# Three row strips side by side, and x, gathers and sums of the first product moved forward

## The chip, the cores and the metric

The kernel runs on one core of a Trainium2 chip. The metric is the device time of an execution in microseconds. The kernel before took 468.69, 468.70 and 470.52 us in three runs, a median of 468.7. One more execution was recorded by the hardware profiler.

## The reference

x has 32 batches of 128 tokens with 512 features. A mask marks up to 32 tokens at the end of each batch. A first half (two small networks) changes only the masked tokens, and a second half, a feed-forward network, changes all of them:

```python
shift, scale, gate_msa = split(silu(t) @ ada_w + ada_b, 3)
norm = where(m, layernorm(x) * (1 + scale) + shift, 0)
fwd = gelu(norm @ ssm_w1 + ssm_b1) @ ssm_w2 + ssm_b2
bwd = gelu(norm @ bwd_w1 + bwd_b1) @ bwd_w2 + bwd_b2
x = x + gate_msa * where(m, fwd + bwd, 0)
shift_mlp, scale_mlp, gate_mlp = split(silu(t) @ ffada_w + ffada_b, 3)
h = gelu_tanh((layernorm(x) * (1 + scale_mlp) + shift_mlp) @ ff_w1 + ff_b1)
out = x + gate_mlp * (h @ ff_w2 + ff_b2)
```

ff_w1 is 512 x 1024 and ff_w2 is 1024 x 512; all is float32. The flips of the reference cancel, token by token.

## The kernel before, in words

*The first half* works on slots. The masked tokens of all batches are numbered, and the first 512 of them fill four tiles of 128 slots, s0 to s3. A matrix `pick` says which batch each slot belongs to, in three copies, each on 32 partitions of its own. The rows of x are gathered by indirect DMAs of GpSimd (`gather_slots`, L270), two tiles at a time. The modulation of all batches (`mod1`: shift in partitions 0 to 31, scale in 32 to 63, gate in 64 to 95) is made once, and `slot_part` (L304) multiplies one of the three strips with that strip of `pick`, so that each slot has its batch's row; each such product takes a PSUM bank of the pool `ps_o` (three banks, tag "o") or `ps_h` (three banks). `modulated` (L177) normalises a tile with two VectorE instructions, which read scale and shift from PSUM. `transposed_slots` (L186) turns it, `hidden` (L193) makes eight blocks of 128 hidden features for two tiles at once, and `project` (L209) multiplies them with w2. For s0 and s1 `finish_slots` (L317) adds gate, bias and x, and writes the rows to `x1_wide` (with mean and variance beside them) and `x1_rows` in DRAM. For s2 and s3 this is done by `with_bias`, `with_gate` and `with_x` (L1246 to L1255), and `with_x` issues the write to `x1_rows`.

*The second half* takes the batches in four pairs, p = 0 to 3, of two sides of four batches. The rows of x are loaded and the masked ones overwritten by gathers from `x1_wide` (pair 0) or `x1_rows` (the others): `take_first_half` (L729), eight indirect DMAs on GpSimd. A gather waits for the load of its tile and for the writes of the rows. `load_side` (L345) loads one side, two transfers of 512 KB on SP's queue.

Both matrix products of the network are made with seven multiplications in place of eight, and the first product twice, one level inside the other. *Outer sums* of the tokens' features are `TokenBlocks.one(j)` (L836; j = 1 to 4, VectorE, 128 x 1024 each), *inner sums* `token_sums(j, n)` (L893; j = 1 to 4, and n = 0 to 3 for the blocks). Sums of the weights (`weight_sums`, L621) are stored to `t_rows` in DRAM (`store_weight_sums`, L633), and `load_weights` (L915) brings them back as `tw`. Outer products run in the order 1, 2, 5, 6, 3, 7, 4, each with inner products P1 to P7. One inner product is a phase of four matmul records (`phase`, L965). `window` (L1063) interleaves phases of two outer products: P5 and P1 of the new one, P3 and P7 of the old one, P2 and P6 of the new one, P4 of the old one. After P5 ScalarE copies the result p5; `with_p5` (L1022) adds it to a kept result on GpSimd; after P6 VectorE adds that to the bank in which P3 goes on accumulating. `fw2_of.combine` makes the sums of ff_w2 that the second product needs.

*Order.* Instructions stand in each engine's queue in the order in which the code names them, and each engine takes its own strictly in that order; a wait holds all that is behind it. Between L1257 and L1301 the order of the first pair is written out by hand; from the loop on it is set by `put(window, phase, function)`, which hangs a function behind a phase. Tiles come from pools with a fixed number of buffers: the tile `spare` (L607) holds sums of weights until they are stored, and the second pair's x goes into it; the other two tiles of that x take the buffers of the gathered slot rows `xc`. PSUM banks turn in the same way, and an allocation waits until the bank's last reader is done. SP issues nearly all direct DMAs, in order.

Of the kernel before, what the change touches and what calls it, by code (L numbers as in the profile page):

```python
# [22 lines left out]
def kernel(  # L23
# [153 lines left out]
    def modulated(src, scale, shift, name, t, stats=None):  # L177

        if stats is None:
            mv, rstd = statistics([src], name)  # L180
            stats = mv[:, 0, 0:1], rstd
        nc.vector.scalar_tensor_tensor(t, src, stats[0], scale, ALU.subtract, ALU.mult)
        nc.vector.scalar_tensor_tensor(t, t, stats[1], shift, ALU.mult, ALU.add)
        return t
# [119 lines left out]
    def slot_part(at, j, pool, tag):  # L304
        return of_slots(pick, at, mod1, j, pool, tag, f"part{j}_s{at}")
# [227 lines left out]
    modulation_matmuls(pm, ada_a, 0, 2, range(KC - 1))  # L533
    gather_slots(find_slots(1, (ps_h, "h")))
    modulation_matmuls(pm, ada_a, 0, 2, range(KC - 1, KC))
    modulation_rows(pm, mod1, modb_a, 0, 2)
    rows = [(slot_part(c, 1, ps_o, "o"), slot_part(c, 0, *((ps_o, "o"), (ps_h, "h"))[c])) for c in range(2)]
    xT_s = ssm.tile([P, KC, NH], F32, tag="xT", name="xT_s0", bufs=2)
    xT_t = ssm.tile([P, KC, NH], F32, tag="xT", name="xT_s1", bufs=2)
    xn = group_of_tiles("s")  # L540
    xn_s = [modulated(xc[c], *rows[c], f"s{c}", xn[:, c]) for c in range(2)]
    fw1 = fwp.tile([P, KC, FF], F32, name="fw1")
# [10 lines left out]
    ada_f = load_ada(ffada_w, "f", 3 * D)  # L553
    for t, vec in ((modb_f, ffada_b), (fb2, ff_b2)):
        broadcast_rows(t, vec, nc.sync)
    nc.sync.dma_start(fw2, ff_w2.rearrange("(k p) f -> p k f", p=P))
    ph_s = {}
# [15 lines left out]
    transposed_slots(xn_s[0], xT_s[:, :, ts(0, P)], "s0")  # L573
    gate_parts = tp.tile([P, D], F32, tag="t", name="gate_parts")
    pm = ps_o.tile([P, 512], F32, tag="o", name="pm_g")
    for k in range(KC):
        nc.tensor.matmul(
            pm[ts(k, B), :], sT[:, k, :], ada_a[:, k, ts(2, D)], start=True, stop=True
        )
    nc.scalar.copy(gate_parts, pm)  # L580
    ptr = ps_t.tile([P, 512], F32, tag="tr", name="ptr_b")
# [4 lines left out]
    nc.vector.tensor_copy(slot_i, ptr[:, n_bias : n_bias + B])  # L586
    hidden_of_tile(0, 0)
    pm = ps_o.tile([P, 512], F32, tag="o", name="pm_gate")
    nc.tensor.matmul(pm[ts(2, B), :], strips, gate_parts, start=True, stop=True)
    modulation_rows(pm, mod1, modb_a, 2, 3)  # L590
    hidden_of_tile(1, 0)
    transposed_slots(xn_s[1], xT_s[:, :, ts(1, P)], "s1")
    hidden_of_tile(2, 0)
# [72 lines left out]
    for f in range(3):  # L666
# [3 lines left out]
        h1.append(t)  # L670
    gs = [keep_gate(c, slot_part(c, 2, ps_o, "o")) for c in range(2)]
    mv_t, rstd_t = statistics(xc[2:], "s23")
    nc.vector.tensor_tensor(b2, b2, b2b, ALU.add)
    b2_row = dram.tile([1, D], F32, name="b2_row")
    for c in range(2):
        with_gated_bias(c, gs[c])
    Weights(fw1, KC // 2, FF // 2, t_1).combine(0, 1, 2, 3)
    h1 += hidden(xT_s, NH, w1, 0, AF.Gelu, "s0", ssm, range(3, HC))
    finish_slots(0, h1, gs[0])
# [5 lines left out]
    finish_slots(1, h1, gs[1])  # L685
    nc.sync.dma_start(b2_row, b2[0:1, :])

    rows = [(slot_part(2 + c, 1, ps_o, "o"), slot_part(2 + c, 0, ps_h, "h")) for c in range(2)]
    mod2 = const.tile([3 * B, D], F32, name="mod2")
    pm = ps_o.tile([P, 512], F32, tag="o", name="pm_f")  # L690
    modulation_matmuls(pm, ada_f, 0, 3, range(KC))
    xn_late = ssm.tile([P, 2, D], F32, tag="xT", name="xn_s_late", bufs=2)
    for c in range(2):
        t = modulated(
            xc[2 + c], *rows[c], f"s{2 + c}", xn_late[:, c], (mv_t[:, c, 0:1], rstd_t[:, c : c + 1])
        )
        transposed_slots(t, xT_t[:, :, ts(c, P)], f"s{2 + c}")
    modulation_rows(pm, mod2, modb_f, 0, 3)
# [506 lines left out]
    take_first_half(0, x_of[0], range(2 * G))  # L1205
    store_weight_sums(1)
    xT = [new_xT(0, side) for side in range(2)]
# [20 lines left out]
    def turn(k):  # L1228
        return lambda: transposed(1, xn_b, xT[1], k)
# [7 lines left out]
    after[4].insert(0, normalised_of_side_0)  # L1237
    after[7] += [lambda: weight_sums(4), normalised_of_side_1]
    h1 = hidden(xT_t, NH, w1, 0, AF.Gelu, "s1", ssm, after=after)
# [16 lines left out]

    po_s2 = project(0, h1, w2, "s2", {2: turn(0), 4: turn(1), 6: turn(2), 7: turn(3)})  # L1257
    of_x[0] = TokenBlocks(0, xT)
    of_x[0].one(1)
    fw2_of.combine(0, 1)  # L1260
    nc.vector.tensor_tensor(fb2_step, fb2[:, D // 2 :], fb2[:, : D // 2], ALU.subtract)
    with_bias(2, po_s2)
    with_gate(2, gs[0])
    with_x(2)
    po = project(1, h1, w2, "s3", bank=(ps_h, "h"))

    store_weight_sums(4, 2)
    with_bias(3, po)
    with_gate(3, gs[1])
    first_half.close()  # L1270
    hp = straight.enter_context(tc.tile_pool(name="hp", bufs=1))
    gp = straight.enter_context(tc.tile_pool(name="gp", bufs=1))
    now = FirstProduct(0, of_x[0].cut(), of_w)
    for j in (1, 2):
        now.load_weights(j)
    now.apart(1)
    for j in (2, 3):
        of_x[0].one(j)
    now.do(1, "P1")
    now.seed(1)  # L1280
    now.do(2, "P1")
    now.do(1, "P5", "P2", "P6")
    of_x[0].one(4)
    now.do(2, "P5")
    now.seed(2)
    now.do(1, "P7")
    now.with_p5(2, "22")
    now.token_sums(1, 0)
    with_x(3)
    x_of[1] = load_x(1, spare)  # L1290
    now.token_sums(1, 1)
    now.do(1, "P3")
    now.with_p5(2, "12")
    now.do(2, "P2", "P6")
    for n in range(2, 4):
        now.token_sums(1, n)
    for n in range(2):
        now.token_sums(2, n)
    now.do(1, "P4")
    for n in range(2, 4):  # L1300
        now.token_sums(2, n)  # L1301
    for p in range(NP):
# [25 lines left out]
        if more_pairs:  # L1328
# [18 lines left out]

            put(*((1, 6) if p else (2, 3)), take_first_half, p + 1, x_next, range(G))
            put(2, 6, take_first_half, p + 1, x_next, range(G, G + 2))
            put(3, 4, take_first_half, p + 1, x_next, range(G + 2, G + 3))  # L1350
            put(5, 4, take_first_half, p + 1, x_next, range(G + 3, 2 * G))
            for i, at in enumerate(((3, 1), (3, 3), (3, 4), (3, 6))):
# [196 lines left out]
```

## Time and profile before

| | |
|---|---|
| median of three runs | 468.7 us |
| profiled execution: time / span | 469.94 / 468.2 us |
| TensorE busy | 452.0 us, 97% |
| VectorE busy | 335.4 us, 72% |
| ScalarE busy | 176.4 us, 38% |
| GpSimd busy | 157.9 us, 34% |
| DMA | 70.95 MB, 152 GB/s on the mean |

The busy time of TensorE takes in half-filled stretches and a slower clock, so a busy engine is not one at its peak. The slots' last projection ends, and the first product begins, at 91.68 us of the span; the second product of pair 0 begins at 138.63 us. In a row of the order of time stand the start, the length, the engine, the line, the operation with the tile written and the tiles read, and in brackets the idle time ahead of it and what ended it.

### The profile page before, as it was taken

What the parts mean: (1) busy time and instruction counts of PE and PEld (TensorE: products, weight loads), DVE (VectorE), ACT (ScalarE), POOL (GpSimd) and SP (SyncE); (2) the same over time, 40 slices, a digit from 0 to 9 for tenths busy, and PEclk for the clock granted to TensorE, in tenths of its full rate; (3) what the DMA queues carried; (4) which work ended last, traced back from release to release, by engine and by line L of the source; (5) the groups of instructions that cost most, each with busy time, mean ns of one, the idle gap of its engine ahead of it and who ended that gap; (6) DMA issues with size and microseconds to landing.
All of it is one profiled execution on the core that took longest, in us unless ns stands there. A gap on an engine that the chain in (4) does not pass through costs nothing.

```text
span 468.2 us, 5888 instructions
## 1 busy us (share of the span) xinstructions
PE 452.0 (97%) x2026; PEld 368.4 (79%) x2026; DVE 335.4 (72%) x549; ACT 176.4 (38%) x381; POOL 157.9 (34%) x147
## 2 busy tenths in 40 slices
PE   6899999999799999999999999999999999999995
PEld 2385377577688888888888888888888887888884
DVE  4678876899469956997687499967873996433645
ACT  3131033544265074254543723544536144562000
POOL 4220171026985000289730004897000025660000
PEclk9899999999899999999999999999999999999999
DMA  8999926194314670944066529230863342212022
GB/s 285 392 392 390 340 96 99 39 357 157 105 66 160 112 114 33 332 149 162 3 202 100 104 88 335 86 142 2 225 96 85 125 168 74 84 77 104 0 81 103
DMA packets 82755, 70.95 MB, mean 152 GB/s; under 512 B 63136, under 2 KB 63664, under 8 KB 81698
## 3 DMA queue, kind: packets, MB, share of 16 engines
q1 hardware_dynamic: 67874, 58.47, 39.7%
q0 software_dynamic: 4064, 10.54, 6.5%
q10 hardware_dynamic: 10784, 1.52, 2.2%
q8 instruction: 17, 0.28, 0.3%
q14 instruction: 16, 0.13, 0.1%
HBM read 56.84 MB, written 13.70 MB: 151 GB/s over the span
## 4 chain that ended last, share of the span: by engine, by line
PE 90%; DVE 3%; DMA 2%; POOL 2%; issue 1%; SPq 0%; ACT 0%; POOLq 0%; DVEq 0%; ACTq 0%
PE a_o L1161 23%; PE e_o L1161 18%; PE a_m L974 17%; PE e_m L974 13%; PE po_s L216 6%; PE ph_s L199 5%; DMA x<-in_x_dram 2%; PE ph_s L564 1%; PE part_s L299 1%; PE pm_ss L279 1%; POOL x L733 1%; PE pm_f L279 1%; PE last L1161 1%; DMA mask_u<-in_mask_BxS_bk_dram 0%; POOL xc L254 0%
## 5 line engine op out<-in xcount | busy, mean ns | idle before, releaser
L1025 POOL TENSOR_TENSOR ha<-p_m,ha 128x512 f32<-128x512 f32 x20 | 26.2, 1310 | 151.4 <-ACT ha L1032 142.0
L1161 PE MATMUL e_o<-fw,ha 128*128 128x256 f32 x256 | 57.9, 379 | 0.0
L796 ACT ACTIVATE xT<-xT,modT 128x128 f32<-128x128 f32 x112 | 44.2, 480 | 31.7 <-DMA xT<-xn 31.6
L1161 PE MATMUL a_o<-t,hb 128*128 128x256 f32 x240 | 54.1, 379 | 0.0
L1161 PEld LDWEIGHTS e_o<-fw,ha 128*128 128x128 f32 x256 | 48.6, 190 | 6.6
L1161 PEld LDWEIGHTS a_o<-t,hb 128*128 128x128 f32 x240 | 45.6, 190 | 6.2
L936 ACT ACTIVATE hb<-hb,biasT 128x256 f32<-128x256 f32 x64 | 29.0, 501 | 28.8 <-POOL hb L1058 19.3
L1025 POOL TENSOR_TENSOR hb<-p_m,hb 128x512 f32<-128x512 f32 x20 | 29.1, 1453 | 27.2 <-DVE hb L1004 26.9
L988 ACT COPY p_m<-e_m 128x512 f32<-128x512 f32 x27 | 15.8, 585 | 47.9 <-PE e_m L974 46.4
L733 POOL DMA_INDIRECT x<-x_rows,slot_i x24 | 28.7, 1194 | 11.9 <-issue 10.6
L1032 ACT COPY ha<-e_m 128x512 f32<-128x512 f32 x32 | 18.5, 578 | 30.9 <-PE e_m L974 27.7
L1161 PE MATMUL a_o<-t,s 128*128 128x256 f32 x128 | 28.9, 379 | 0.0
L1161 PE MATMUL a_o<-fw,ha 128*128 128x256 f32 x128 | 28.9, 379 | 0.0
L1161 PE MATMUL e_o<-fw,s 128*128 128x256 f32 x128 | 28.9, 379 | 0.0
L999 DVE TENSOR_TENSOR e_m<-a_m,ha 128x512 f32<-128x512 f32 x20 | 13.9, 697 | 20.4 <-POOL ha L1025 9.5
L216 PE MATMUL po_s<-w,h_s 128*128 128x512 f32 x64 | 28.5, 592 | 0.0
L1161 PEld LDWEIGHTS a_o<-t,s 128*128 128x128 f32 x128 | 24.3, 190 | 3.3
L1161 PEld LDWEIGHTS a_o<-fw,ha 128*128 128x128 f32 x128 | 24.3, 190 | 3.3
L1161 PEld LDWEIGHTS e_o<-fw,s 128*128 128x128 f32 x128 | 24.3, 190 | 3.3
L936 ACT ACTIVATE ha<-e_m,biasT 128x256 f32<-128x256 f32 x48 | 20.0, 468 | 14.5 <-PE e_m L974 12.0
L974 PE MATMUL a_m<-xT,tw 128*128 128x256 f32 x96 | 24.6, 379 | 0.0
L1004 DVE TENSOR_TENSOR hb<-a_m,hb 128x512 f32<-128x512 f32 x20 | 13.7, 685 | 14.3 <-PE a_m L974 14.3
(226 smaller groups left out, 904.6 us busy)
## 6 DMA issues: line engine op xcount, KB each, us to landing
tw<-t_rows SPq DMA_DIRECT2D x16, 896.0 KB, 5.3
x<-in_x_dram SPq DMA_DIRECT2D x16, 512.0 KB, 7.5
gate<-gate_rows POOLq DMA_DIRECT2D x8, 1024.0 KB
out_dram<-x SPq DMA_DIRECT2D x15, 512.0 KB, 3.9
xT<-xn SPq DMA_DIRECT2D x92, 64.0 KB, 2.4
fw<-in_L_cond_ff_w_dram SPq DMA_DIRECT2D x2, 2048.0 KB
ada_f<-in_L_cond_ffada_w_dram SPq DMA_DIRECT2D x4, 768.0 KB, 16.2
ada_a<-in_L_cond_ada_w_dram SPq DMA_DIRECT2D x4, 512.0 KB, 3.7
```

The costliest lines, as they stand in the source:

```text
L199: nc.tensor.matmul(ph[:, :n], w[:, k, ts(f, P)], xT[:, k, :], start=(k == 0), stop=(k == KC - 1))
L216: nc.tensor.matmul(po, h[f][:, ts(i, P)], w[:, f, :], start=(f == 0), stop=(f == HC - 1))
L733: nc.gpsimd.indirect_dma_start(out=raw[i // 2][:, i % 2] if p == 0 else xs[i // G][i % G // 2][:, i % 2], out_offset=None, in_=x1_rows if ...
L796: nc.scalar.activation(out, src, AF.Identity, bias=shift, scale=scale)
L936: nc.scalar.activation(dst[:, n], src[:, n], AF.Gelu_apprx_tanh, bias=biasT[:, f : f + 1])
L974: nc.tensor.matmul(bank[:, ts(n, QT)], self.w_block(j, product)[:, ts(n, P)], self.x_block(j, product), start=(product in ("P1", "P5") and ...
L988: nc.scalar.copy(p5, e)
L999: nc.vector.tensor_tensor(e, a, p5, add)
L1004: nc.vector.tensor_tensor(dst, a, dst if prior else self.p5[j], add)
L1025: nc.gpsimd.tensor_tensor(self.place(RESULT[j], c), self.p5[j], other, ALU.add)
L1032: nc.scalar.copy(self.place(RESULT[j], c), src)
L1161: nc.tensor.matmul(part, src[:, k, ts(i, P)], w[product][:, k, :], start=(last and k == 0), stop=True, skip_group_check=True,)
```

## The change

Names are as above.

- The gates' matmuls `pm_g` stand in front of the first tile's transposes, in a bank of `ps_t`. The statistics of s0 are issued ahead of the second pair of `gather_slots`.
- `fb2` and `fw2` are loaded behind the writes of the first slot rows instead of with the other weights.
- `gate_and_next_tile(c)` makes the gate of tile c and scale and shift of tile 2 + c together, in three banks of `ps_o`, and normalises tile 2 + c at once, into `spare[1]`. It is called before hidden block 3 and behind block 6. The transposes of s2 and s3 then stand ahead of `pm_f`.
- Of the weight sums, `normalised_of_side_1` goes ahead of the fourth, all three stores stand together behind it, and behind these the loads of the second pair's first side. The first `turn` stands ahead of the projection of s2.
- The outer sums `one(2)` to `one(4)` are made before `with_bias(3)`, `with_x(3)` directly behind `with_gate(3)`, then the loads of the second side, and only then those of `tw`. The inner sums (1, n) come ahead of the first phase, (2, n) together behind `with_p5(2, "22")`. The combination of ff_w2 moves behind the phases written out by hand.
- All eight `take_first_half` of the second pair stand behind `with_p5(2, "12")` instead of in windows 2, 3 and 5.

```diff
-    gather_slots(find_slots(1, (ps_h, "h")))
+    token_i = find_slots(1, (ps_h, "h"))
     modulation_matmuls(pm, ada_a, 0, 2, range(KC - 1, KC))
     modulation_rows(pm, mod1, modb_a, 0, 2)
     rows = [(slot_part(c, 1, ps_o, "o"), slot_part(c, 0, *((ps_o, "o"), (ps_h, "h"))[c])) for c in range(2)]
+    gate_parts = tp.tile([P, D], F32, tag="t", name="gate_parts")
+    pm = ps_t.tile([P, 512], F32, tag="tr", name="pm_g")
+    for k in range(KC):
+        nc.tensor.matmul(
+            pm[ts(k, B), :], sT[:, k, :], ada_a[:, k, ts(2, D)], start=True, stop=True
+        )
+    nc.scalar.copy(gate_parts, pm)
...
-    xn_s = [modulated(xc[c], *rows[c], f"s{c}", xn[:, c]) for c in range(2)]
+    mv, rstd = statistics(xc[:1], "s0")
+    gather_slots(token_i)
+    xn_s = [
+        modulated(xc[0], *rows[0], "s0", xn[:, 0], (mv[:, 0, 0:1], rstd)),
+        modulated(xc[1], *rows[1], "s1", xn[:, 1]),
+    ]
...
-    for t, vec in ((modb_f, ffada_b), (fb2, ff_b2)):
-        broadcast_rows(t, vec, nc.sync)
-    nc.sync.dma_start(fw2, ff_w2.rearrange("(k p) f -> p k f", p=P))
+    broadcast_rows(modb_f, ffada_b, nc.sync)
...
     transposed_slots(xn_s[0], xT_s[:, :, ts(0, P)], "s0")
-    gate_parts = tp.tile([P, D], F32, tag="t", name="gate_parts")
-    pm = ps_o.tile([P, 512], F32, tag="o", name="pm_g")
...
-    nc.scalar.copy(gate_parts, pm)
...
     hidden_of_tile(0, 0)
+    hidden_of_tile(1, 0)
+    transposed_slots(xn_s[1], xT_s[:, :, ts(1, P)], "s1")
     pm = ps_o.tile([P, 512], F32, tag="o", name="pm_gate")
     nc.tensor.matmul(pm[ts(2, B), :], strips, gate_parts, start=True, stop=True)
     modulation_rows(pm, mod1, modb_a, 2, 3)
-    hidden_of_tile(1, 0)
-    transposed_slots(xn_s[1], xT_s[:, :, ts(1, P)], "s1")
     hidden_of_tile(2, 0)
...
-    gs = [keep_gate(c, slot_part(c, 2, ps_o, "o")) for c in range(2)]
     mv_t, rstd_t = statistics(xc[2:], "s23")
+    xn_late = []
+
+    def gate_and_next_tile(c):
+        gs.append(keep_gate(c, slot_part(c, 2, ps_o, "o")))
+        rows = slot_part(2 + c, 1, ps_o, "o"), slot_part(2 + c, 0, ps_o, "o")
+        xn_late.append(
+            modulated(
+                xc[2 + c], *rows, f"s{2 + c}", spare[1][:, c], (mv_t[:, c, 0:1], rstd_t[:, c : c + 1])
+            )
+        )
+
+    gs = []
+    gate_and_next_tile(0)
     nc.vector.tensor_tensor(b2, b2, b2b, ALU.add)
     b2_row = dram.tile([1, D], F32, name="b2_row")
-    for c in range(2):
-        with_gated_bias(c, gs[c])
+    with_gated_bias(0, gs[0])
+    h1 += hidden(xT_s, NH, w1, 0, AF.Gelu, "s0", ssm, range(3, HC - 1))
+    gate_and_next_tile(1)
     Weights(fw1, KC // 2, FF // 2, t_1).combine(0, 1, 2, 3)
-    h1 += hidden(xT_s, NH, w1, 0, AF.Gelu, "s0", ssm, range(3, HC))
+    with_gated_bias(1, gs[1])
+    h1 += hidden(xT_s, NH, w1, 0, AF.Gelu, "s0", ssm, range(HC - 1, HC))
     finish_slots(0, h1, gs[0])
...
     nc.sync.dma_start(b2_row, b2[0:1, :])
-
-    rows = [(slot_part(2 + c, 1, ps_o, "o"), slot_part(2 + c, 0, ps_h, "h")) for c in range(2)]
+    broadcast_rows(fb2, ff_b2, nc.sync)
+    nc.sync.dma_start(fw2, ff_w2.rearrange("(k p) f -> p k f", p=P))
+
+    for c in range(2):
+        transposed_slots(xn_late[c], xT_t[:, :, ts(c, P)], f"s{2 + c}")
     mod2 = const.tile([3 * B, D], F32, name="mod2")
     pm = ps_o.tile([P, 512], F32, tag="o", name="pm_f")
     modulation_matmuls(pm, ada_f, 0, 3, range(KC))
-    xn_late = ssm.tile([P, 2, D], F32, tag="xT", name="xn_s_late", bufs=2)
-    for c in range(2):
-        t = modulated(
-            xc[2 + c], *rows[c], f"s{2 + c}", xn_late[:, c], (mv_t[:, c, 0:1], rstd_t[:, c : c + 1])
-        )
-        transposed_slots(t, xT_t[:, :, ts(c, P)], f"s{2 + c}")
     modulation_rows(pm, mod2, modb_f, 0, 3)
...
     take_first_half(0, x_of[0], range(2 * G))
-    store_weight_sums(1)
...
-    after[7] += [lambda: weight_sums(4), normalised_of_side_1]
+    after[7] += [
+        normalised_of_side_1,
+        lambda: weight_sums(4),
+        lambda: store_weight_sums(1, 2, 4),
+        lambda: x_of.update({1: [load_side(1, 0, spare), None]}),
+        turn(0),
+    ]
...
-    po_s2 = project(0, h1, w2, "s2", {2: turn(0), 4: turn(1), 6: turn(2), 7: turn(3)})
+    po_s2 = project(0, h1, w2, "s2", {2: turn(1), 4: turn(2), 6: turn(3)})
     of_x[0] = TokenBlocks(0, xT)
     of_x[0].one(1)
-    fw2_of.combine(0, 1)
-    nc.vector.tensor_tensor(fb2_step, fb2[:, D // 2 :], fb2[:, : D // 2], ALU.subtract)
     with_bias(2, po_s2)
     with_gate(2, gs[0])
     with_x(2)
     po = project(1, h1, w2, "s3", bank=(ps_h, "h"))
-
-    store_weight_sums(4, 2)
+    for j in (2, 3, 4):
+        of_x[0].one(j)
     with_bias(3, po)
     with_gate(3, gs[1])
+    with_x(3)
     first_half.close()
...
+    x_of[1][1] = load_side(1, 1)
     now = FirstProduct(0, of_x[0].cut(), of_w)
     for j in (1, 2):
         now.load_weights(j)
+    for n in range(4):
+        now.token_sums(1, n)
     now.apart(1)
-    for j in (2, 3):
-        of_x[0].one(j)
     now.do(1, "P1")
     now.seed(1)
     now.do(2, "P1")
     now.do(1, "P5", "P2", "P6")
-    of_x[0].one(4)
     now.do(2, "P5")
     now.seed(2)
     now.do(1, "P7")
     now.with_p5(2, "22")
-    now.token_sums(1, 0)
-    with_x(3)
-    x_of[1] = load_x(1, spare)
-    now.token_sums(1, 1)
+    for n in range(4):
+        now.token_sums(2, n)
     now.do(1, "P3")
     now.with_p5(2, "12")
+    take_first_half(1, x_of[1])
     now.do(2, "P2", "P6")
-    for n in range(2, 4):
-        now.token_sums(1, n)
-    for n in range(2):
-        now.token_sums(2, n)
     now.do(1, "P4")
-    for n in range(2, 4):
-        now.token_sums(2, n)
+    fw2_of.combine(0, 1)
+    nc.vector.tensor_tensor(fb2_step, fb2[:, D // 2 :], fb2[:, : D // 2], ALU.subtract)
...
-            put(*((1, 6) if p else (2, 3)), take_first_half, p + 1, x_next, range(G))
-            put(2, 6, take_first_half, p + 1, x_next, range(G, G + 2))
-            put(3, 4, take_first_half, p + 1, x_next, range(G + 2, G + 3))
-            put(5, 4, take_first_half, p + 1, x_next, range(G + 3, 2 * G))
+            if p:
+                put(1, 6, take_first_half, p + 1, x_next, range(G))
+                put(2, 6, take_first_half, p + 1, x_next, range(G, G + 2))
+                put(3, 4, take_first_half, p + 1, x_next, range(G + 2, G + 3))
+                put(5, 4, take_first_half, p + 1, x_next, range(G + 3, 2 * G))
```

More of the change, by code (lines that the diff above doesn't have):

```diff
@@ L573 @@
     transposed_slots(xn_s[0], xT_s[:, :, ts(0, P)], "s0")
-    gate_parts = tp.tile([P, D], F32, tag="t", name="gate_parts")
-    pm = ps_o.tile([P, 512], F32, tag="o", name="pm_g")
-    for k in range(KC):
-        nc.tensor.matmul(
-            pm[ts(k, B), :], sT[:, k, :], ada_a[:, k, ts(2, D)], start=True, stop=True
-        )
-    nc.scalar.copy(gate_parts, pm)
     ptr = ps_t.tile([P, 512], F32, tag="tr", name="ptr_b")
@@ L691 @@
     modulation_matmuls(pm, ada_f, 0, 3, range(KC))
-    xn_late = ssm.tile([P, 2, D], F32, tag="xT", name="xn_s_late", bufs=2)
-    for c in range(2):
-        t = modulated(
-            xc[2 + c], *rows[c], f"s{2 + c}", xn_late[:, c], (mv_t[:, c, 0:1], rstd_t[:, c : c + 1])
-        )
-        transposed_slots(t, xT_t[:, :, ts(c, P)], f"s{2 + c}")
     modulation_rows(pm, mod2, modb_f, 0, 3)
```

## The prediction

> **What bounds the kernel now.** I read four views in this order: the page's busy times and slices, TensorE in order of time, the stretches at a finer grain, and GpSimd and the chain around the one long gap.
>
> The page first:
>
> ```profile
> PE 452.0 (97%) x2026; PEld 368.4 (79%) x2026; DVE 335.4 (72%) x549; ACT 176.4 (38%) x381; POOL 157.9 (34%) x147
> PE   6899999999799999999999999999999999999995
> PEclk9899999999899999999999999999999999999999
> ```
>
> TensorE is the bound: its work does not change, so only its holes can be won. They lie in slices 1, 2 and 11, and in 2 and 11 the granted clock is lower too; the order of time shows them (start, us, what, idle before it and who ended it):
>
> ```profile
> 17.16 0.66 PE L190 MATMUL ptr_s<-ident,xn_s 128*128 128x128 f32 x4 [1.27 <-DVE xn_s L183]
> 17.75 1.67 PE L577 MATMUL pm_g<-ada_a,sT 128*32 128x512 f32 x8
> 28.03 1.98 PE L299 MATMUL part_s<-mod,pick 32*128 32x512 f32 x4
> 52.50 1.99 PE L299 MATMUL part_s<-mod,pick 32*128 32x512 f32 x8
> 59.86 1.99 PE L199 MATMUL ph_s<-xT_s,w 128*128 128x256 f32 x8 [0.78 <-ACT xT_s L191]
> 120.43 2.06 PE L974 MATMUL e_m<-xn_sy,tw 128*128 128x256 f32 x4 [2.55 <-DVE e_m L999]
> 122.29 1.82 PE L974 MATMUL a_m<-xn_sy,tw 128*128 128x256 f32 x4
> ```
>
> A phase of the first product (four records) normally takes 0.864 us from start to start; the last two rows take double. The clock says why (stretch, length, PE busy, granted clock, DMA):
>
> ```profile
> 14.66:18.08 3.42, 2.15 (x14) 1.00 1.05 388
> 18.08:21.49 3.41, 3.41 (x18) 0.50 1.04 401
> 117.06:120.48 3.42, 0.87 (x5) 1.00 0.85 268
> 120.48:123.90 3.42, 3.42 (x8) 0.50 0.07 21
> ```
>
> Twice a stretch with a hole is followed by 3.41 us at half clock, a further 1.7 us lost each. From 124 us on TensorE stands once, for 0.77 us. Behind the gap at 117.8 stands GpSimd, whose adds wait behind row gathers, which wait for x:
>
> ```profile
> 103.01 7.63 DMA x<-in_x_dram
> ...
> 117.35 1.00 POOL x L733
> 118.37 1.28 POOL ha L1025
> 119.68 0.71 DVE e_m L999
> 120.43 2.06 PE e_m L974 x4
> ```
>
> [...]here VectorE's add of 128x512 took 1.75 us at 99.80 and 101.47 beside GpSimd's adds, 0.68 otherwise.
>
> **The change, part by part.** Times on the profile's clock; S is the end of the slots' last projection, 91.68 before.
>
> *Opening.* The first tile's statistics go ahead of the second pair of gathers on GpSimd. Its root takes 0.59 and can start at 15.05 (ve_s ends 15.01) instead of 15.73, so xn_s is ready at 16.6 instead of 17.1. The gate matmuls pm_g move in front of the transposes, into the hole: 15.85 to about 16.8 (1.6 measured mostly at half clock; 0.9 at full). Transposes 0.44, then the bias transposes wait for ScalarE's copy of pm_g (0.59) in the same bank: 17.5; the copy of xT_s follows it, so hidden blocks start at 18.1. Two blocks 0.95 each, transposes 0.44, pm_gate 0.88, a block 0.95, pt 0.15: pt at 22.35 instead of 25.03. Gain 2.7, of which 1.7 is the half clock, which should not come[...]. The second gathers issue 1 us later; their rows are first read at 33 us, and that costs nothing.
>
> *Parts.* Gate, scale and shift of a slot tile lie in three row strips. Before: 1.91 (28.0) plus 1.92 (52.5) = 3.83. After: twice about 0.96, if three run abreast: gain 1.9. Bounds: 0.86 each at best, 1.72 if only two do (gain 0.4). But the second triple comes after four hidden blocks, at pt+0.13+2.88+0.96+6.91 = pt+10.9, and needs banks which VectorE frees only after all the statistics: before, ve_s ended at 35.74, the root at 36.89, so the normalising add ends at pt+12.65. The last part ends at pt+13.55, the projections at pt+29.0, against 27.5 before. So the stall is 1.5 and goes on the path: the last hidden block and both projections stand behind it on TensorE. Behind it on VectorE stand fw1's combinations, which the load holds until 39.5 anyway, to 44.5; two more adds and finish_slots(0) at 45.9 against 45.74. Then transposes come ahead of pm_f, whose 3.56 us cover ScalarE's copies: 0.78 and a little, 0.9 gained. Sum to here: 2.7 - 1.5 + 1.9 + 0.9 = 4.0, S at 87.7.
>
> *What is moved on the queues, to S.* fb2 and fw2 (2.3 MB) leave the busy stretch and go to SP's queue behind x1_wide; they then run beside the first pair's eight gathers (57 to 67.5, 1.3 us each); the first normalisation reads them from 63. Idle DMA hides them (share 0.11 at 58 to 60, 0.13 at 64 to 68); fw2's combination reads them at 100; without that cover VectorE would wait there, with the add of P7 of outer product 2 queued behind. The three stores of weight sums (2.7 MB at some 390 GB/s, 7 us) and half of the second pair's x (1 MB) follow the 16 turned copies, which land at 77.3; the stretch 80 to 92 had a share of 0.08. They end near 84.5 and 87; one(4), which overwrites a stored tile, starts at 86.2. If the stores were 2 us later, the sums after S would be too. turn(0) in front of the projection needs normalised rows at 72; VectorE, with the weight sums behind them, has them at 69.5. Cost nothing.
>
> *First product.* Before, VectorE was filled from S to S+25. After: the sums one(2) to one(4), 3 x 1.22, end at 87.4, just ahead of S. After S: the last slots' three ops to S+2.3, four sums to S+4.6, then the products' first add as before. with_x(3) ends at S+2.3 instead of S+9.9. Behind it SP issues the rows, 1 MB of x, and only then the first weights tw (0.9 MB); 2.2 MB at 390 GB/s plus about 1.5 us put them at S+9.8; P5 of outer product 5 reads them at S+9.9. I take 0; up to 1 if late, half of which the add for P3(2) would hide: it is at S+12.4, as before[...]. fw2's combination (2 x 1.22 + 0.42) takes the place of one(4) and with_x, so VectorE is within +-0.5 of before until S+25.
>
> *Gathers.* All eight stand on GpSimd right behind its two adds, at S+11.0, instead of six from S+17.1 waiting for x. Pair 1 gives their price, beside the same VectorE work:
>
> ```profile
> 199.58 1.36 POOL L733 DMA_INDIRECT x<-x_rows,slot_i  x1 [0.17 <-issue]
> ...
> 206.84 1.49 POOL L733 DMA_INDIRECT x<-x_rows,slot_i  x1 [0.30 <-ACT p_m L988]
> 208.36 1.28 POOL L1025 TENSOR_TENSOR ha<-p_m,ha 128x512 f32<-128x512 f32 x1
> ```
>
> Six took 8.8 us, 1.46 each; eight take 11.7, to S+22.7. GpSimd's add (1.28) ends at S+24.0, VectorE's at S+24.7. TensorE reaches that phase (the 28th, 27 x 0.864 = 23.3 at the least, about 3 us lost to VectorE as before) at S+26.4; before it was S+28.75. Gain 2.35, plus 1.7 of half clock that a hole this small does not bring: 4.05. The two later gathers are gone from between the adds, so GpSimd keeps ahead.
>
> From pair 1 on nothing changes; TensorE carries the gain to the end. Sum 4.0 + 4.05 = 8.0: span 468.2 to 460.2. The profiled execution took 469.94, 1.74 around its span, so 461.9. The median, 468.7, is 1.24 below that execution; as one or the other half-clock stretch may fall differently in the other runs, I take 7.7 from it: 461.0.
>
> **The rivals.** *A: only the opening's gain.* The first product ends as late as before, through tw behind x on SP's queue, or VectorE later than I have it. For: VectorE is full there. Against: the hole is ended by GpSimd, not VectorE. 468.7 - 4.0 = 464.7.
> *B: only the first product's gain, or half the opening's.* The strips don't go abreast (1.5 lost) or the second triple's stall, with only a quarter of the array busy, brings a half-clock stretch (1.7). Against: lone parts at 28 and 62 us brought none. 461.0 + 2.4 = 463.4.
> *C, slower: the gathers shut the adds out.* Eight in a row stand before the add for outer product 6. The first two of before took 1.83 and 2.02 (2.1 to 2.3 with the issue) while VectorE ran sums back to back; here it also runs the 1.22 us combinations. It ties when that phase starts at S+28.75+4.0, when GpSimd is free at S+30.8, or 2.5 us a gather. At 3.0 it is S+35, another 4.2 us late: 473. Against: pair 1's 1.46.
> *D: nothing measurable,* if C's price is near its tie: 468.7.
>
> **Numbers.** The likeliest case 0.62 (its own range 459.0 to 463.2), A 0.15, B 0.12, C 0.07, D 0.04. The range 458.4 to 466.8 holds all but C, D and the tails. About 0.5%, 2.3 us, is what a measurement of this kernel can tell from no change: faster is the likeliest, A and B, 0.88 with a little of A lost; same 0.05; slower 0.07.
>
> **What would show it.** Right: no half clock at 18; pt near 22.4; parts in two triples, the second with a wait of VectorE's add; no wait for xT_s at 59; projections ending at 87.7; gathers from about 99 to 110; no hole over 1 us behind them. Wrong: tw landing after P5(5) wants it, GpSimd's add still the releaser of a long hole, parts one after the other, or one(4) waiting for a store.

## The result, and the profile after

The changed kernel took 465.5 us (median of 8 runs, 464.29 to 467.49) beside 469.46 us for the kernel before (8 runs): a ratio of 0.992, 95% interval 0.9895 to 0.9943. It is faster, by 4.0 us where 7.7 were forecast. The profiled span fell from 468.2 to 465.0 us. The page after:

```profile
PE 448.7 (97%) x2026; PEld 367.2 (79%) x2026; DVE 334.5 (72%) x549; ACT 176.3 (38%) x381; POOL 157.1 (34%) x147
PE   6799999979999999999999999999999999999995
PEclk9899999999899999999999999999999999999999
```

The hole of slice 11 is gone and a smaller one stands in slice 9; the clock of slice 2 is still low. Some rows of TensorE in order of time (the columns are those of before):

```profile
17.06 0.66 PE L190 MATMUL ptr_s<-ident,xn_s 128*128 128x128 f32 x4 [1.21 <-DVE xn_s L183]
24.50 0.20 PE L645 MATMUL pt<-count,every 32*128 32x1 bf16 x2
27.50 1.13 PE L299 MATMUL part_s<-mod,pick 32*128 32x512 f32 x6
35.67 2.26 PE L299 MATMUL part_s<-mod,pick 32*128 32x512 f32 x6
...
94.09 1.03 PE L988 MATMUL e_m<-s,fw 128*128 128x256 f32 x4
96.96 1.13 PE L988 MATMUL a_m_alone<-xT,t 128*128 128x256 f32 x4 [1.84 <-DVE e_m L1013]
102.63 1.10 PE L988 MATMUL e_m<-sx,tw 128*128 128x256 f32 x4 [1.08 <-DMA tw<-t_rows]
117.28 1.03 PE L988 MATMUL e_m<-xn_sy,tw 128*128 128x256 f32 x4
```

The first product begins (S) at 89.78. Inner product P7 of outer product 1 is written P7(1) from here on, and the others likewise. Two stops are new: at P7(1), 2.0 us longer than a phase (0.15 before), and at P5(5), 1.25 longer (0 before, but 0.8 one phase later). The phase of the old gap, P3(6), starts at 117.28, with no gap and at full clock; before it was 120.43 at half clock. A half-clock stretch stays in the opening (stretch, length, TensorE busy, clock, DMA):

```profile
15.84:19.25 3.41, 1.72 (x15) 1.00 0.95 341
19.25:22.66 3.41, 3.41 (x16) 0.50 1.01 376
93.00:96.40 3.40, 2.12 (x10) 1.00 0.45 131
```

VectorE ahead of the two stops, and SP's queue:

```profile
90.88 1.23 DVE L857 TENSOR_TENSOR s<-xT,s 128x1024 f32<-128x1024 f32 x1 [1.95 <-DMA t_rows<-tw]
93.46 0.69 DVE L1273 TENSOR_TENSOR t_s<-t_s,xc 128x512 f32<-128x512 f32 x1
96.21 0.69 DVE L1013 TENSOR_TENSOR e_m<-a_m_alone,p_m 128x512 f32<-128x512 f32 x1
```

```profile
84.56 1.56 SPq L639 DMA_DIRECT2D t_rows<-tw  x1
86.21 2.18 SPq L351 DMA_DIRECT2D x<-in_x_dram  x2
88.45 6.08 SPq L1274 DMA_DIRECT2D x_rows<-t_s  x2
94.57 0.98 SPq L351 DMA_DIRECT2D x<-in_x_dram  x2
95.66 0.88 SPq L934 DMA_DIRECT2D tw<-t_rows  x2
```

The sum one(4) (L857) waits 1.95 us for the store of the tile that it overwrites. All behind it on VectorE is late: with_x(3) (L1273), the last step of the slots' rows, and on SP the write of these rows, x, and tw behind x. The chain of waits, in order of time, says what the last of these costs:

```profile
95.66 6.83 DMA tw<-t_rows
102.49 0.14 issue
102.63 1.10 PE e_m L988 x4
```

GpSimd's gathers, finally, cost nearly what was forecast, 12.6 us for eight (11.7):

```profile
102.37 1.32 POOL L747 DMA_INDIRECT x<-x_rows,slot_i  x1 [0.16 <-issue]
...
113.98 1.00 POOL L747 DMA_INDIRECT x<-x_rows,slot_i  x1 [0.30 <-issue]
115.00 1.28 POOL L1039 TENSOR_TENSOR ha<-p_m,ha 128x512 f32<-128x512 f32 x1
```

### The profile page after: what moved, and what is told of

Same layout as the page of the kernel before. It is cut to its first block, busy times and chain, and to the rows that moved or that the text cites. A ratio compares the mean times of both kernels' runs of the same rounds, so it can differ in the third digit from the quotient of the medians.

```text
span 465.0 us, 5878 instructions
## 1 busy us (share of the span) xinstructions
PE 448.7 (97%) x2026; PEld 367.2 (79%) x2026; DVE 334.5 (72%) x549; ACT 176.3 (38%) x381; POOL 157.1 (34%) x147
## 4 chain that ended last, share of the span: by engine, by line
PE 76%; DVE 6%; DMA 6%; SPq 3%; POOL 3%; ACT 3%; issue 2%; DVEq 0%; POOLq 0%; ACTq 0%
PE a_o L1175 17%; PE a_m L988 16%; PE e_o L1175 13%; PE e_m L988 12%; PE po_s L216 6%; PE ph_s L199 5%; SPq L827 3%; DMA tw<-t_rows 3%; PE ph_s L574 2%; DMA xc<-in_x_dram,token_i_s 1%; ACT xT L810 1%; DMA xT<-xn 1%; PE part_s L299 1%; PE pm_f L279 1%; PE last L1175 1%
## 5 line engine op out<-in xcount | busy, mean ns | idle before, releaser
L1013 DVE TENSOR_TENSOR e_m<-a_m,ha 128x512 f32<-128x512 f32 x20 | 13.9, 697 | 18.1 <-POOL ha L1039 6.7
L988 PE MATMUL e_m<-s,fw 128*128 128x256 f32 x92 | 23.7, 380 | 0.0
```

The lines of the kernel that those rows point to most:

```text
L988: nc.tensor.matmul(bank[:, ts(n, QT)], self.w_block(j, product)[:, ts(n, P)], self.x_block(j, product), start=(product in ("P1", "P5") and ...
L1013: nc.vector.tensor_tensor(e, a, p5, add)
```

## The experiments

All were run beside the kernel before, whose medians in the four groups were 469.52, 469.35, 469.54 and 469.34; each group ran on a chip of its own, so that kernels of different groups are compared by their ratios. Two causes were open: transfers beside the first gathers (fw2) make the rows, and all behind them, late (theory 1), or the order on SP's queue does, with three stores in a block and tw behind x (theory 2). Later runs ask what each part of the change is worth. The table gives the median of several executions, and from the one that was profiled the start of the small matmul `pt` that closes the opening, S, and the start of with_x(3) on VectorE, of P5(5) and of P3(6), in us. "The first normalisation" is that of pair 0's first tile, which needs the gathered rows (L770); the "turned copies" are the DMA copies behind it (L827); a "triple" is gate, scale and shift made in three row strips.

| kernel | median | ratio, 95% | pt | S | with_x(3) | P5(5) | P3(6) |
|---|---|---|---|---|---|---|---|
| before | | | 25.03 | 91.68 | 99.80 | 101.69 | 120.43 |
| changed, first | 465.5 | 0.9895-0.9943 | 24.50 | 89.78 | 93.46 | 102.63 | 117.28 |
| e0 changed, again | 464.66 | 0.9873-0.9914 | 22.51 | 87.79 | 91.87 | 101.47 | 116.03 |
| e1 fw2 early | 463.55 | 0.9854-0.9893 | 22.74 | 89.30 | 90.95 | 99.69 | 115.05 |
| e2 hole filled | 464.69 | 0.9878-0.9919 | 22.96 | 88.43 | 91.66 | 100.30 | 115.49 |
| e3 triple later | 465.14 | 0.9878-0.9920 | 23.12 | 88.55 | 92.38 | 101.67 | 116.31 |
| f0 opening back | 466.15 | 0.9901-0.9948 | 24.61 | 89.99 | 93.86 | 102.97 | 117.67 |
| f1 gathers back | 469.44 | 0.9980-1.0011 | 22.58 | 88.72 | 92.67 | 101.19 | 122.36 |
| f2 store 1 back | 462.72 | 0.9831-0.9874 | 22.61 | 88.20 | 91.18 | 100.42 | 115.06 |
| f3 fw2 early, tw first | 462.68 | 0.9832-0.9870 | 22.71 | 88.99 | 90.65 | 98.76 | 114.75 |
| g0 parts back | 463.68 | 0.9850-0.9896 | 22.91 | 89.52 | 91.23 | 100.62 | 115.25 |
| g1 sums behind | 465.06 | 0.9895-0.9938 | 23.07 | 88.35 | 92.30 | 101.57 | 116.24 |
| g2 store 1, tw, sums | 464.79 | 0.9873-0.9919 | 22.48 | 88.09 | 89.90 | 98.54 | 116.67 |
| h0 parts, fw2, tw | 463.73 | 0.9856-0.9893 | 22.77 | 89.37 | 91.02 | 99.13 | 115.13 |

**e0: the changed kernel once more.**

> The changed kernel once more, as the reference for the three beside it on the same chip. Both theories: about 465.5, 0.8% under the kernel before. In its profile, theory 1 (the load of fw2 beside the first pair's gathers makes everything up to the first product late) expects the wait of some 2.7 us ahead of the first normalisation again, and the stop of TensorE of 1.5 to 2 us at P7 of outer product 1; theory 2 (SP's order of stores, x and tw alone is what is late) expects those stops, whether or not the first normalisation waits.

464.66 us. Its profile has no hole and no half clock in the opening, and S is where the forecast had it, but the stop at P7(1) is there, and now a half-clock stretch follows it:

```profile
22.51 0.20 PE L645 MATMUL pt<-count,every 32*128 32x1 bf16 x2
87.79 1.03 PE L988 MATMUL a_m_alone<-xT,fw 128*128 128x256 f32 x4
95.36 1.42 PE L988 MATMUL a_m_alone<-xT,t 128*128 128x256 f32 x4 [2.23 <-DVE e_m L1013]
```

```profile
92.60:96.01 3.41, 1.18 (x6) 1.00 0.71 250
96.01:99.42 3.41, 3.41 (x10) 0.51 1.03 401
```

So S was gained as forecast, and much of it lost again behind S: with_x(3) starts 4.1 us after S (3.7 in the first execution), where the forecast's end of S+2.3 means S+1.6. The waits ahead of it, on VectorE and then the stores on SP (the first issue, and the last from its issue to its landing):

```profile
65.81 0.55 DVE L770 TENSOR_SCALAR xn<-x 128x512 f32<-128x512 f32 x1 [2.79 <-DMA x<-x_wide,slot_i]
89.28 1.23 DVE L857 TENSOR_TENSOR s<-xT,s 128x1024 f32<-128x1024 f32 x1 [2.29 <-DMA t_rows<-tw]
```

```profile
78.06 0.84 SPq L638 DMA_DIRECT2D t_rows<-x  x1
82.71 6.45 DMA t_rows<-tw
```

Both stops of theory 1 are there, and so are those of theory 2: this run alone doesn't part them.

**e1: fw2 and its bias loaded where before loaded them.**

```diff
-    broadcast_rows(modb_f, ffada_b, nc.sync)
+    for t, vec in ((modb_f, ffada_b), (fb2, ff_b2)):
+        broadcast_rows(t, vec, nc.sync)
+    nc.sync.dma_start(fw2, ff_w2.rearrange("(k p) f -> p k f", p=P))
...
-    broadcast_rows(fb2, ff_b2, nc.sync)
-    nc.sync.dma_start(fw2, ff_w2.rearrange("(k p) f -> p k f", p=P))
```

> Only the loads of fw2 and fb2 go back among the weights. Theory 1 (fw2 beside the gathers): the first normalisation no longer waits, so the turned copies, the stores, the last outer sum and with_x(3) come some 2.5 us earlier; the stop of 1.84 us at P7 of outer product 1 and most of that of 1.08 us for tw go, and the time falls by 1.5 to 2.5 us against the changed kernel. Theory 2 (SP's order alone): the stops stay within 0.5 us and the time is within 0.5 us of the changed kernel, or a little longer, since the write of the slot rows stands behind fw2 again.

463.55, 1.1 less than e0, between the two bands. The first normalisation starts at 63.15, without a wait, where it started at 65.81 in e0 after waiting 2.79; one(4) waits no more, and P7(1) stops 0.16. But the first gather is issued later, at 60.06 instead of 58.67 (5.0 us behind the issue of the rows' second write, 3.8 in e0; fw2 ahead of that write on SP's queue may be why, which was not tested). The last gathers now come beside the turned copies, which start earlier, and TensorE waits for their rows:

```profile
74.08 0.33 PE L816 MATMUL ptr<-ident,xn 128*128 128x128 f32 x1 [1.07 <-DVE xn L770]
```

S is 1.5 later than in e0, and with it with_x(3), which now waits for the projection alone (S+1.65). Theory 1 is right on the rows and on one(4), but the time gained is smaller than expected.

**e2: the hole of the opening filled** with one matmul of 128x512, which nothing reads.

```diff
+    fill = ps_t.tile([P, 512], F32, tag="tr", name="fill")
+    nc.tensor.matmul(fill, ident, ada_a[:, 0, :512], start=True, stop=True)
```

> One more matmul of 128x512 (0.86 us), whose result nobody reads, stands in the hole of 1.2 us between the gates' matmuls and the first transposes. If the hole brings the half clock at 19 us: no half-clock stretch there, pt (the small count matmul) at 22.8 instead of 24.5, and a time 1.2 to 1.7 us under the changed kernel. If it comes from something else (few rows of the array in use, the start of the program): the half clock stays, and the time is within 0.5 us.

464.69, nothing gained. The half clock of the opening is not in this profile, but nor is it in e0's or in any later one with the changed opening, so the run doesn't tell whether the hole brings it. And although the three stores stand in one block here too, one(4) waits for none of them in this profile, but 0.72 us for ScalarE (L812).

**e3: the second triple of parts behind the last hidden block.**

```diff
-    h1 += hidden(xT_s, NH, w1, 0, AF.Gelu, "s0", ssm, range(3, HC - 1))
+    h1 += hidden(xT_s, NH, w1, 0, AF.Gelu, "s0", ssm, range(3, HC))
     gate_and_next_tile(1)
...
-    h1 += hidden(xT_s, NH, w1, 0, AF.Gelu, "s0", ssm, range(HC - 1, HC))
```

> The second triple of gate, scale and shift moves from behind hidden block 6 to behind block 7, when VectorE has read the first triple. If the triple's length of 2.26 us is the wait for the banks: it takes 1.1 us there, the projections start 1.2 us earlier, and the time falls by about 1.1 us against the changed kernel. If three strips take that long by themselves in this place: no change.

465.14, not told apart from e0: the time is that of the second case, the triple that of the first. It falls from 2.25 to the 1.13 of the first triple, so the excess was the wait for banks; the projection then waits for the gate:

```profile
36.02 1.13 PE L299 MATMUL part_s<-mod,pick 32*128 32x512 f32 x6
37.81 4.56 PE L216 MATMUL po_s<-w,h_s 128*128 128x512 f32 x10 [0.66 <-ACT gs L309]
```

**f0: the opening alone undone** (statistics, gathers, pm_g and pm_gate as before).

```diff
...
-    mv, rstd = statistics(xc[:1], "s0")
-    gather_slots(token_i)
-    xn_s = [
-        modulated(xc[0], *rows[0], "s0", xn[:, 0], (mv[:, 0, 0:1], rstd)),
-        modulated(xc[1], *rows[1], "s1", xn[:, 1]),
-    ]
+    xn_s = [modulated(xc[c], *rows[c], f"s{c}", xn[:, c]) for c in range(2)]
...
```

> The changed kernel with its opening alone undone (statistics, gathers, pm_g and pm_gate where they stood). The changed kernel measured 464.7 beside 469.5. If the opening's gain is mostly the forecast's 2.7 us, half clock included, and the profile of the changed kernel (0.5) was the exception: 466.5 to 467.4, pt near 25.0. If a half-clock stretch falls in the opening of most executions of both, the opening is worth about 0.5: 465.0 to 465.4.

466.15, 1.5 above e0: just under the first band, and the intervals overlap a little. In the profiles S and P3(6) are 2.2 and 1.6 later, and a half-clock stretch stands in the opening again (17.0 to 20.4). The opening is worth some 1.5 us.

**f1: the second pair's gathers back in windows 2, 3 and 5,** with x still loaded early.

```diff
-    take_first_half(1, x_of[1])
...
-            if p:
-                put(1, 6, take_first_half, p + 1, x_next, range(G))
+            put(*((1, 6) if p else (2, 3)), take_first_half, p + 1, x_next, range(G))
```

(and likewise the other three calls of `put`.)

> The changed kernel with the second pair's gathers put back into the second product's fill-ins of before, x still loaded early. As forecast, the move is worth 2.35 us and a half-clock stretch of 1.7: 467 to 468.8, with a hole behind GpSimd's add near S+28. If the first product of the changed kernel is held elsewhere, at P7(1), and the gathers no longer decide, the time stays: 464.3 to 465.3. Between the two, if only the add's place counts and no half clock comes: 465.8 to 466.8.

469.44, above all three bands: no gain is left, and against e0 the move carries 4.8 us. But the hole that comes back has another cause than the one before: x has long been there, and a sum on VectorE (L927) takes 4.03 us beside three of GpSimd's adds that now follow each other without a pause:

```profile
111.09 1.27 POOL L1039 TENSOR_TENSOR ha<-p_m,ha 128x512 f32<-128x512 f32 x1
112.32 1.26 POOL L1039 TENSOR_TENSOR hb<-p_m,hb 128x512 f32<-128x512 f32 x1
113.54 1.25 POOL L1068 TENSOR_TENSOR ha<-ha 128x512 f32<-128x512 f32 x1
```

```profile
111.33 4.03 DVE L927 TENSOR_TENSOR xT<-xT,xn_sy 128x512 f32<-128x512 f32 x1
116.42 0.66 DVE L1018 TENSOR_TENSOR hb<-a_m,p_m 128x512 f32<-128x512 f32 x1
```

TensorE stands 3.68 us, waiting for the add `hb` (L1018) behind that sum, and then has two half-clock stretches (115.3 to 122.2). So the 4.8 us are no test of the forecast's 4.05, in which the gathers wait for x; what the move is worth with x loaded late was not run.

**f2: the first of the three stores back beside the first gathers.**

```diff
     take_first_half(0, x_of[0], range(2 * G))
+    store_weight_sums(1)
...
-        lambda: store_weight_sums(1, 2, 4),
+        lambda: store_weight_sums(2, 4),
```

> The changed kernel with the first of the three stores of weight sums (0.9 MB) back beside the first pair's gathers, fw2's load left where the change put it. If the hole at P7(1) comes from the three stores that stand in one block behind the turned copies, the wait of one(4) shrinks from 2.3 us to at most 0.5 and the time falls to about 463.5. If it comes from transfers beside the gathers that make the rows late, 0.9 MB more there (2.3 us at 390 GB/s) delays the first normalisation, and the time stays or rises: 464.7 to 466.

462.72, 1.9 less than e0, and the intervals just touch: as theory 2 has it. The 0.9 MB beside the gathers cost the rows hardly anything (first normalisation 65.99 against 65.81), and one(4) no longer waits for a store but 0.71 for ScalarE:

```profile
85.52 1.23 DVE L857 TENSOR_TENSOR s<-s,xT 128x1024 f32<-128x1024 f32 x1 [0.95 <-DMA t_rows<-tw]
88.59 1.23 DVE L857 TENSOR_TENSOR s<-xT,s 128x1024 f32<-128x1024 f32 x1 [0.71 <-ACT xT L810]
```

The time carries this more than the profile does: e2's one(4), with the stores in a block, also waited only for ScalarE, and the profiled execution of f2 took 463.56, longer than its median. But f2's interval lies below e2's.

**f3: fw2 early, tw of outer product 1 ahead of the second side's x,** and the `turn`s of side 1 one matmul later each.

The edit of e1, and:

```diff
-    x_of[1][1] = load_side(1, 1)
...
         now.load_weights(j)
+        if j == 1:
+            x_of[1][1] = load_side(1, 1)
...
-        turn(0),
-    po_s2 = project(0, h1, w2, "s2", {2: turn(1), 4: turn(2), 6: turn(3)})
+    po_s2 = project(0, h1, w2, "s2", {1: turn(0), 3: turn(1), 5: turn(2), 6: turn(3)})
```

> The changed kernel with fw2 and its bias loaded early again (463.55 measured), and also tw of outer product 1 ahead of the second side's x on SyncE's queue, and the first slot transposes of side 1 a block later, behind the first matmul of the projection. If tw behind x is what is left at P5(5), and the wait of 1.07 us for the normalised rows is lost time: 462.0 to 462.8. If x, later by tw's 0.9 MB, then holds the gathers or other waits take their place: 463.3 to 464.

462.68, inside the band of tw, though not told apart from e1 (the intervals overlap, and the two profiled executions took 463.01 and 463.25). And P5(5) starting at 98.76, 0.9 earlier than in e1 and with no wait, is not what brought it: VectorE's add for the second phase behind is next to be late, so is its `hb` further on, and P3(6) is only 0.3 earlier, as S is:

```profile
98.76 1.03 PE L987 MATMUL e_m<-sx,tw 128*128 128x256 f32 x4
101.23 1.13 PE L987 MATMUL e_m<-s,fw 128*128 128x256 f32 x4 [0.58 <-DVE e_m L1012]
...
112.06 1.13 PE L987 MATMUL a_m<-sx,tw 128*128 128x256 f32 x4 [0.33 <-DVE hb L1017]
```

f2 and f3 are the fastest versions, 6.6 and 6.7 us below the kernel before.

**g0: parts and transposes of s2 and s3 put back.**

```diff
+    gs = [keep_gate(c, slot_part(c, 2, ps_o, "o")) for c in range(2)]
     mv_t, rstd_t = statistics(xc[2:], "s23")
...
-    gate_and_next_tile(0)
...
-    gate_and_next_tile(1)
...
+    rows = [(slot_part(2 + c, 1, ps_o, "o"), slot_part(2 + c, 0, ps_h, "h")) for c in range(2)]
...
```

> The changed kernel with the parts and the slots' second transposes alone put back (both gates ahead of the statistics, scale and shift after the projections, pm_f in front of the transposes). As forecast, the parts give 1.9, less a stall of 1.5, and the copies of xT_s behind pm_f 0.9, so 1.3 in all: 466.0, S near 89.1 in an execution whose pt is near 22.5. If the second triple's wait (1.1 us more than the first) and its late projections eat it: 464.3 to 465.0.

463.68, below both bands. By the medians the kernel is 1.0 faster without the parts; the intervals overlap, but a loss of 1.3 us lies outside them. S is later by just what was forecast: it stands 66.6 us behind pt, 65.3 in e0, a difference of 1.3. But with no stall in front of the projections the rows of the first slots leave earlier; from pt to their second write are 30.8 us, 32.3 in e0. one(4) waits 0.49 instead of 2.29, and with_x(3) starts 0.6 earlier than in e0 although S is 1.7 later. The rows' second write on SP, in e0 and then in g0:

```profile
54.85 0.32 SPq L323 DMA_DIRECT2D x_wide<-t_s  x1
```

```profile
53.71 0.32 SPq L323 DMA_DIRECT2D x_wide<-t_s  x1
```

**g1: the inner sums (1, n) behind the two first adds.** (The expectation calls them outer sums; they are those of `token_sums`.)

```diff
-    for n in range(4):
-        now.token_sums(1, n)
     now.apart(1)
...
     now.seed(2)
+    for n in range(4):
+        now.token_sums(1, n)
```

> The changed kernel with the four outer sums of the first pair (2.2 us of VectorE) moved from ahead of the first add of the products to behind the two first adds. Everything ahead of S stays, so one(4) still waits about 2.3 us for the store. If P7(1) stops because this late queue of VectorE stands ahead of its add, the stop falls from 2.4 to about 0.3. If tw, then as late as before, takes its place at P5(5), that stop grows from nothing or 1.25 to about 2 and the time falls only to 464.0 to 464.7; without such a wait 462.5.

465.06, just above the first band. P7(1) stops 0.78 instead of 2.39, and nothing is won; P5(5) waits for tw until the same time:

```profile
94.31 1.13 PE L988 MATMUL a_m_alone<-xT,t 128*128 128x256 f32 x4 [0.62 <-DVE e_m L1013]
101.57 1.10 PE L988 MATMUL e_m<-sx,tw 128*128 128x256 f32 x4 [2.61 <-DMA tw<-t_rows]
```

The stop at P7(1) alone decides nothing.

**g2: f2 with tw first and the sums behind.** (The three edits are those shown at f2, f3 without the `turn`s, and g1.)

> The changed kernel with the first store back beside the first pair's gathers (462.7 measured for it alone), tw of outer product 1 ahead of the second side's x, and the outer sums behind the two first adds. It left 1.29 at P7(1) and 1.33 at P5(5). If these two are the rest of what the forecast did not see: both under 0.3, and 460.5 to 461.5. If GpSimd and VectorE behind them are full, as the sums for P2(2) at S+12.4 in the forecast, other waits of 0.5 to 0.8 take their place: 461.7 to 462.6.

464.79, outside both bands. P5(5) is the earliest of all (98.54), but the sums now stand in front of VectorE's later adds: TensorE stops 2.2 us for one of them (L1013) at 102.46, and the three phases from there to 106.84 are 0.5 to 0.85 us longer, which I take for a half-clock stretch (the mean clock of this execution is 0.995, as in e0; 1.000 in h0). Beside f2's 462.72, the early place of the sums was worth having.

**h0: g0 with fw2 early and tw first.** (The edits are those of g0 and e1 and the first of f3.)

> The changed kernel with the parts put back (463.7 measured for it alone), fw2 and its bias loaded early again, and tw of outer product 1 ahead of the second side's x. If what decides behind S is when the chain from the slots' rows to tw ends (rows stored, gathered, turned, stores, x, tw) and no longer when TensorE reaches S: with the chain's start 1.1 us earlier and its bytes out of the way, the stops at P5(5) (1.34) and in front of the first turned tile (1.07) go, and the time is 462.0 to 462.6 although S is as late as 89.5. If S counts as in the forecast, the 1.3 us that the parts give are missing: 463.3 to 464.3.

463.73, in the band of the other view. Both waits went, as I had it (P5(5) at 99.13 without one), and still nothing was won on g0. With the stores out of the way with_x(3) stands 1.65 us behind S, here as in e1 and f3, and the late S of 89.37 then counts.

**What they give together.** In the profiled executions the start of with_x(3) orders the times, from 463.01 us (f3) to 466.05 (f0), but for neighbours up to 0.25 us apart, the first execution (466.70), which lost 1.1 us much later, and f1 and g2, whose edits hold later adds. P3(6) stands 23.8 to 24.2 us behind it in all of the changed kernels but these two. Three queues lead through this stretch:

- SP's: rows, x, tw, P5(5), and from there TensorE; in the first execution 2.2 + 7.0 + 14.65 = 23.8, of which TensorE stands still once, 0.33 us for VectorE.
- VectorE's: from with_x(3) it is idle once, for 0.6 to 0.9 us, up to the add `hb` (L1018) for which TensorE has that wait, 2.7 us ahead of P3(6).
- GpSimd's: behind an earlier `hb` of VectorE two adds, the eight gathers and three adds, with pauses of at most about 0.3 us (98.96 to 118.72 in the first execution), up to a sum for which TensorE waits 0.34 us, 2.2 us behind P3(6).

The last two waits stand, equally long and at the same distance from P3(6), in all eleven profiles without f1 and g2, whether tw was early or late. So VectorE's and GpSimd's queues end last; in the first execution SP's ends about half a microsecond before. That is why tw first, or the sums in another place of VectorE's queue, shortens nothing; an earlier with_x(3) shortens all three. And with_x(3) has two conditions: the projection (S+1.65) and one(4), which waits for the store of the tile that it overwrites, and so for rows, gathers, turned copies and stores, or for ScalarE, which scales the turned copies (0.71 and 0.72 us in f2 and e2). In the changed kernel's two profiles the store makes the second the later by 2.0 to 2.4 us.

## Why the prediction was wrong on the size

*Opening: right at pt, except in the one execution first recorded.* The forecast had pt at 22.35; the eleven later profiles with the changed opening have it at 22.5 to 23.1, without half clock. In the first recorded one the first tile's rows came late, TensorE had its hole (1.21 us ahead of the transposes), and half clock followed (a clock of 0.50 from 19.25 to 22.66): 0.5 gained instead of 2.5. That the half clock would not come was my estimate; how large a hole brings one, no run shows.

```profile
14.37 0.69 DVE L155 BATCH_NORM_STATS2 st_s<-xc 128x6 f32<-128x512 f32 x1 [1.56 <-DMA xc<-in_x_dram,token_i_s]
```

In the time the runs put the whole at about 1.5 of the forecast's 2.7 (f0), with overlapping intervals.

*Parts: right to S, wrong behind it.* Two triples took 1.13 and 2.25, for 0.96 and 2.5 with the wait; the projections start 15.2 us behind pt (15.1 forecast), xT_s is not waited for, S is 87.79 in e0 (87.7). But I put the stall of 1.5 on TensorE alone. Behind the projections stand also the rows of the first slots, the gathers and all that SP does after them; with the stall these are 1.5 later (g0), and they were the later condition of with_x(3). The 1.3 won at S are not in the time.

*"Cost nothing" for what is moved on the queues: this is the step that failed.* I had the first normalisation at 63, the stores' end at 84.5, one(4) at 86.2. In e0 the first normalisation waits for its rows until 65.81 (e1, without fw2's load beside the gathers: 63.15), the last store is issued at 82.71 and lands at 89.16, and one(4) starts at 89.28. The term that was most mis-sized is the stores': 7 us for 2.7 MB, beginning at 77.3, where e0 has 11.1 us from the first issue (78.06) to the last landing. The text said "if the stores were 2 us later, the sums after S would be too"; they were 4.7 later, and with_x(3) ended at S+4.8 instead of S+2.3. The three stores in one block (f2) and the load beside the gathers (e1) both have a part in it; the two edits were not run together. Two of the forecast's signs of being wrong came true, one(4) waiting for a store and tw landing after P5(5) wants it; GpSimd's add as the releaser of a long hole did not.

*First product.* These 2.5 us are what is missing at with_x(3). The forecast had the way from with_x(3) to P3(6) 0.6 too long (S+26.4 where S+25.75 is measured with the stores out of the way), so P3(6) is 1.9 late: 116.03 for 114.1. "tw lands at S+9.8 ... I take 0" was wrong by itself too: in the first execution it landed 8.3 us behind the end of with_x(3), not 7.5, of which the 1.5 beyond the bytes were my estimate. But with tw early no more was won that the runs can tell (f3, h0), so 0 was its price, for a reason the forecast did not give: VectorE's queue ends later than SP's. The nearest rival is A, 464.7 through "tw behind x on SP's queue, or VectorE later than I have it": right that both are late, wrong that only the opening's gain is left.

*Gathers: the price right, the gain not shown as forecast.* Eight took 12.6 us for 11.7, and GpSimd's add ended no long hole. Without the move the whole gain is gone (f1), but by another mechanism; that its 4.8 us lie near the forecast's 4.05 is luck. Of the 1.7 for the half clock behind, 1.2 came: a wait of 0.5 follows P3(6). Rival C, gathers of over 2.5 us, is out at 1.58 each, issue included; B's half-clock stretch did come, but in the first product, behind P7(1), or in the opening, not at the second triple.

*The sum on e0's profile:* to S 3.9 (forecast 4.0), S to P3(6) 0.5 (2.35), the half clock behind 1.2 (1.7), the rest -0.2: 5.4 where 8.0 were forecast. In the first recorded execution it is 1.9, 1.25, 1.2 and -1.1. Two waits in the last pair's first product stand in that execution and neither in e0 nor before: 0.28 for VectorE at 374.51 and 0.42 for tw at 396.95. They may be that last 1.1; why they came is open.

*Open:* why the stores took 11.1 us; and why the first normalisation is delayed by 2 MB of fw2 ahead of the rows but not by 0.9 MB more behind it (f2). That the bytes' place in the queue decides it is argued, not shown.

## What to carry to other kernels

When work is moved to idle queues, follow each line to the instruction where it meets the bounding engine's own, and compare the times there: here S and the stores met at with_x(3), and what was won on S was lost on the stores. Bytes over a rate were too short a price for six stores in a row on one queue: 11.1 us, not 7. A stall priced on the bounding engine also delays what leaves it for DRAM and comes back, here by 1.5 us (g0). Where several lines of nearly equal length lead to a phase, look for the instruction that all start from.

## What the hardware showed unasked

- Where a half-clock stretch falls is not a property of the kernel: the changed kernel had it at 19.25 in one recorded execution and at 96.01 in the other, 3.41 us long each time, behind 3.41 us in which TensorE was busy for 1.72 and 1.18 us. The busy share alone doesn't decide it: in the first of these executions TensorE was busy for 1.58 of the 3.42 us from 94.34 to 97.76, and the clock in the 3.41 us behind was 1.00, while in the kernel before 2.15 of 3.42 us busy (14.66 to 18.08) were followed by 3.41 us at 0.50.
- Three products of 32 partitions each, in three row strips, take 1.13 us together (x6), where two in one strip take 1.98 (before, at 28.03) and four in two strips 1.99 (before, at 52.50).
- One VectorE sum of 128x512 took 4.03 us beside three GpSimd adds in a row (f1), 0.68 otherwise; beside GpSimd's two adds in the kernel before it took 1.75.
- The last of the three pairs of stores landed 6.45 us after its issue with five other stores ahead of it on SP's queue (e0), and the first load of tw 6.8 us after its own (first execution, 95.66).
